# A GRU scan on one core: half of each block copied by ScalarE, a slot of its own for z's last products, a new written order

## The chip, the core and the metric

The kernel runs on one core of one Trainium2 chip. The metric is the time of the device in microseconds (us) for one execution of the whole program; lower is better. The figure given for a kernel is the median of its runs, with the lowest and the highest beside it.

A core has five engines that work side by side, each through its own list of instructions in a fixed order: TensorE (PE; its weight loads are listed apart as PEld), VectorE (DVE), ScalarE (ACT), GpSimd (POOL) and SyncE (SP), which here only issues DMAs. They share SBUF, the large on-chip memory, and PSUM, the accumulators of TensorE (here eight banks). Semaphores tell an engine that another has finished what it needs.

## The reference

```python
def step(h, inp):                       # h: 64 x 512
    x_t, prop = inp
    comb = jnp.concatenate([x_t, h], axis=-1)
    z = jax.nn.sigmoid(comb @ Wz + bz)
    r = jax.nn.sigmoid(comb @ Wr + br)
    comb2 = jnp.concatenate([x_t, r * h], axis=-1)
    h_cand = jnp.tanh(comb2 @ Wh + bh)
    h_new = (1.0 - z) * h + z * h_cand
    h_next = jnp.where(prop, jnp.tanh(h_new @ Wp + bp), h_new)
    return (h_next, h_new)
...
_, ys = jax.lax.scan(step, h0, (xs, do_prop))   # do_prop: every 4th step but the last
...
x = x + ys                              # x: 64 x 128 x 512, float32
```

The batch has 64 sequences of 128 steps, and the input and the state have 512 numbers each. W is 1024 x 512 for each of the three gates (its upper half meets x_t, its lower half h), Wp is 512 x 512. Everything is float32.

## The kernel before

**Two kinds of work.** The products of x with the upper halves of the weights don't depend on the recurrence. They are made in batches of four steps, ahead of time, by a scheme of the Strassen kind: seven products where eight would be plain, nested twice, so that GpSimd first sums blocks of x (`s12r`, `s56`, `o12` and the like, 128 columns each), VectorE and GpSimd have once summed the weights (`weigh`, L560, into `tw`, `tt`, `tf`), and TensorE multiplies sums by sums into four PSUM banks (`ps_q`, `ps_y`, `ps_a`, `ps_x`). ScalarE and VectorE bring the products to SBUF (`mb`); GpSimd adds them up, 768 columns at a time (`pool_add`, L796, 1.83 us each), into a staging tile `st`. The recurrent part, h times the lower halves, has to run step after step.

**Layout.** The batch is cut into two halves, e and l, of 32 rows each. The state of one half is a tile of 128 partitions (four quarters of the 512 features, 32 batch rows each) by 128 columns. Its transpose `hT` is what TensorE takes as the stationary operand. One product of a gate for one half is 16 matmuls of 128 columns, or 8 where half of the features are meant. All matmuls are issued by `mm` (L397), so in the profile they are told apart by their tiles.

**From the staging tile to the place of use.** A block of x's gates leaves GpSimd in `st` with the batch halves on the wrong partitions. `place` (L807) issues four DMAs from SP (L813), 64 partitions by 384 columns each, which put it into `cp`: two of them change the half of the partitions, two keep it. `cp` is what the gates add in.

**One step.** Steps 0 to 3 and 124 to 127 multiply plainly (`gates_plain`). Steps 4 to 123 (`gates_seven`) make r and z of both halves with seven products of 8 matmuls. GpSimd makes the four sums or differences of `hT` for it (`sa`, L999). Four of the products go, one after another, through one PSUM slot, B_ in `ps_b`: the first from `hT` itself, three from `sa`; E_ and A_, R_ are slots in `ps_b`, `ps_e` and `ps_r`. VectorE adds the products and x's part together (`plus`, L1006): for z it forms c3 = E_ + x and ps_z = B_ + c3 for one half, then, after the next product has come into B_, ps_z = B_ + x for the other. Then comes `rest`: ScalarE's sigmoid of z (L955), VectorE's keep = (z - 1) * h (L1043), the products of the third gate from `rhT` into `ps_e` and `ps_r`, tanh into `cand`, and for each half

```python
tensor(lambda h=h, zh=zh: nc.vector.tensor_mul(zh, cand_(t)[:, h, :], zh),
...
tensor(lambda h=h, zh=zh, n=n: nc.vector.tensor_sub(h_(n)[:, h, :], zh, keep_(t)[:, h, :]),
...
turn(hT_(n)[:, h, :], h_(n)[:, h, :], [("h", n, h)], [("hT", n, h)])
```

in the profile L1057, L1071 and, inside `turn`, L908. Here zh is a part of `ps_z`, in PSUM; cand, keep and h are in SBUF. The next step's first product waits for that transpose. After every fourth step, h goes through Wp and tanh first. GpSimd adds h to x (L1088) and SP writes the result to the output.

**What sets the order.** Every operation is announced with what it reads and writes. A table of numbers (`ORDER`) then says in which order all operations are emitted, and each engine runs its own in just that order; the program derives the semaphore waits from the reads and writes. So the products of the batches stand between those of the recurrence at places that the table has fixed. TensorE's list opens with 42 dummy matmuls (`idle`) that need no data. SP's list opens with loads of x (`load_step`, `load_x`) and of the weights (`load_wx` for the upper halves, `load_wh` for the lower ones).

## Time and profile before

| what | value |
|---|---|
| median of 3 runs | 1272.42 us (1270.58 to 1274.52) |
| the profiled execution | 1273.74 us |
| its span, first to last instruction | 1271.9 us |
| mean granted clock of TensorE | 0.998 of full speed |
| PE busy | 1239.7 us, 97%, 37698 instructions |
| PEld busy | 1109.9 us, 87% |
| VectorE busy | 822.3 us, 65%, 2567 instructions |
| ScalarE busy | 677.1 us, 53%, 2063 instructions |
| GpSimd busy | 939.3 us, 74%, 1481 instructions |
| DMA | 95.9 MB, mean 75 GB/s |

The profile's page comes from one execution. Times are in us unless ns is written. A row such as "L796 POOL TENSOR_TENSOR st<-mb,mb 128x768 ... x77 | 141.3, 1834 | 30.2 <-ACT mb L763 24.6" is a group of alike instructions: line 796 of the kernel, the engine, the operation, what is written and what read, partitions by columns, and the count; then the busy time and the mean of one in ns; then how long the engine had stood idle just ahead of them, and what ended most of that. In the view of waits, a row names engine, tile and line that waited, then what released them, with the time in us, the count and the longest. In the timeline a row is start, duration, engine, line and tiles, and in square brackets the wait ahead of it. Consecutive matmuls overlap in the records, so "busy" for TensorE says that one was in flight and not that it ran at its best.

### The profile page before, as it was taken

How to read it: one execution, taken by the hardware profiler on the slowest of the kernel's cores; microseconds unless marked ns; L12 is line 12 of the kernel's file. 1: busy time of each engine (PE TensorE's matmuls, PEld its weight loads, DVE VectorE, ACT ScalarE, POOL GpSimd, SP SyncE). 2: the span in 40 equal slices, each digit the busy share in tenths (PEclk: the TensorE clock that was granted, in tenths of full speed). 3: DMA queues.
4: the chain of work that ended last, by engine and by line, in shares of the span. 5: the costliest groups of instructions: out<-in, count | busy, mean ns of one | idle time of the engine just before them, and what ended most of it. 6: DMA issues, size and time to landing. Idle time of an engine off the chain costs nothing. (4 is left out here: it accounts for less than half of the span.)

```text
span 1271.9 us, 85560 instructions
## 1 busy us (share of the span) xinstructions
PE 1239.7 (97%) x37698; PEld 1109.9 (87%) x37698; DVE 822.3 (65%) x2567; ACT 677.1 (53%) x2063; POOL 939.3 (74%) x1481
## 2 busy tenths in 40 slices
PE   8899999999999999999999999999999999999987
PEld 6788888888889998888889888998988988898877
DVE  4566666666666666666676666666666666666654
ACT  1355655555555555655555555564655555555543
POOL 7767777788677887767878676887777877677851
PEclk9999999999999999999999999999999999999999
DMA  8322232322232332222322232322232322233221
GB/s 217 85 68 64 62 83 66 87 72 63 73 75 69 86 74 68 62 73 76 82 69 64 71 76 76 86 62 71 67 80 71 84 68 61 75 75 77 70 70 37
DMA packets 112002, 95.90 MB, mean 75 GB/s; under 512 B 10891, under 2 KB 107531, under 8 KB 111630
## 3 DMA queue, kind: packets, MB, share of 16 engines
q1 hardware_dynamic: 110760, 89.76, 28.1%
q8 instruction: 296, 4.85, 1.6%
q0 software_dynamic: 512, 0.53, 0.2%
q14 instruction: 76, 0.62, 0.2%
q10 hardware_dynamic: 358, 0.14, 0.0%
HBM read 24.84 MB, written 16.78 MB: 33 GB/s over the span
## 5 line engine op out<-in xcount | busy, mean ns | idle before, releaser
L999 POOL TENSOR_TENSOR sa<-hT 128x64 f32<-128x64 f32 x240 | 75.9, 323 | 119.7 <-DVE hT L908 107.9
L796 POOL TENSOR_TENSOR st<-mb,mb 128x768 f32<-128x768 f32 x77 | 141.3, 1834 | 30.2 <-ACT mb L763 24.6
L397 PE MATMUL ps_b<-wh,sa 128*32 128x128 f32 x3840 | 155.4, 274 | 3.7 <-DVE ps_r L1006 1.6
L1088 POOL TENSOR_TENSOR xj<-xj,h 128x256 f32<-128x256 f32 x127 | 93.7, 738 | 66.3 <-DVE h L1071 65.1
L397 PE MATMUL ps_r<-wh,rhT 128*32 128x128 f32 x4096 | 140.9, 274 | 1.5 <-issue 1.5
L397 PE MATMUL ps_e<-wh,rhT 128*32 128x128 f32 x4096 | 138.9, 273 | 2.0 <-ACT ps_e L951 1.5
L397 PEld LDWEIGHTS ps_b<-wh,sa 128*32 128x32 f32 x3840 | 109.2, 109 | 29.3 <-issue 15.6
L796 POOL TENSOR_TENSOR mb<-mb,mb 128x768 f32<-128x768 f32 x60 | 110.0, 1834 | 32.3 <-ACT mb L763 27.6
L397 PEld LDWEIGHTS ps_e<-wh,rhT 128*32 128x32 f32 x4096 | 117.1, 110 | 8.0 <-DVE rhT L908 2.5
L397 PEld LDWEIGHTS ps_r<-wh,rhT 128*32 128x32 f32 x4096 | 119.5, 110 | 4.2 <-issue 1.9
L908 DVE STREAM_TRANSPOSE hT<-h 128x128 f32<-128x128 f32 x318 | 96.6, 307 | 31.0 <-ACT h L955 19.7
L518 DVE STREAM_TRANSPOSE xT<-xj 128x256 f32<-128x256 f32 x128 | 84.1, 661 | 40.9 <-DMA xj<-in_x_dram 37.3
L397 PE MATMUL ps_y<-tw,s 128*32 128x192 f32 x1456 | 93.6, 326 | 0.0
L1043 DVE SCALAR_TENSOR_TENSOR keep<-ps_z,h 128x256 f32<-128x256 f32 x128 | 54.3, 424 | 57.0 <-ACT ps_z L955 57.0
L796 POOL TENSOR_TENSOR st<-mb 128x768 f32<-128x768 f32 x47 | 86.6, 1842 | 4.7 <-DMA cp<-st 3.2
L397 PE MATMUL ps_e<-wh,hT 128*32 128x128 f32 x2176 | 85.2, 273 | 2.1 <-ACT ps_r L951 1.4
L1057 DVE TENSOR_TENSOR ps_z<-cand,ps_z 128x128 f32<-128x128 f32 x256 | 74.2, 290 | 18.2 <-ACT cand L955 6.8
L999 POOL TENSOR_TENSOR sa<-hT,sa 128x64 f32<-128x64 f32 x240 | 77.5, 323 | 10.8
L951 ACT COPY ps_r<-cp 128x128 f32<-128x128 f32 x256 | 69.5, 271 | 28.0 <-PE ps_r L397 12.3
L908 DVE STREAM_TRANSPOSE rhT<-rh 128x128 f32<-128x128 f32 x256 | 79.2, 309 | 6.8
L397 PE MATMUL ps_b<-wh,hT 128*32 128x128 f32 x1920 | 78.0, 276 | 4.9 <-DVE hT L908 3.5
L955 ACT ACTIVATE ps_z<-ps_z 128x256 f32<-128x256 f32 x128 | 47.1, 368 | 60.6 <-DVE ps_z L1006 53.7
(173 smaller groups left out, 3388.4 us busy)
## 6 DMA issues: line engine op xcount, KB each, us to landing
cp<-st SPq DMA_DIRECT2D x496, 96.0 KB
out_dram<-xj SPq DMA_DIRECT2D x254, 64.0 KB
xj<-in_x_dram SPq DMA_DIRECT2D x248, 64.0 KB
wh<-in_L_cond_Wr_dram SPq DMA_DIRECT2D x4, 256.0 KB
wx<-in_L_cond_Wh_dram SPq DMA_DIRECT2D x2, 512.0 KB
wx<-in_L_cond_Wz_dram SPq DMA_DIRECT2D x2, 512.0 KB
wh<-in_L_cond_Wz_dram SPq DMA_DIRECT2D x4, 256.0 KB
wh<-in_L_cond_Wh_dram SPq DMA_DIRECT2D x4, 256.0 KB
```

The source lines that it names most:

```text
L397: nc.tensor.matmul(dst, lhsT=lhsT, rhs=rhs, start=start, stop=True, skip_group_check=True)
L518: lambda: nc.vector.transpose(out=xT_(g)[:, i].rearrange("p c (a h b) -> p h (c a) b", a=S, h=S), in_=xj(t).rearrange("p h (e k) -> p h k ...
L796: el("pool", 768, lambda: nc.gpsimd.tensor_add(dst, a, b), reads, writes, rank=FOLD)
L908: add("dve", 0.23, lambda: nc.vector.transpose(out=dst, in_=src), reads, writes, land=0.08, main=True)
L951: el("act", n, lambda: nc.scalar.copy(dst, src), reads, writes, "+" + bank, main=True)
L955: el("act", n, lambda: nc.scalar.activation(dst, src, func), reads, writes, used_, main=True)
L999: tensor(lambda: nc.gpsimd.tensor_sub(sa[:, n], a, b), reads, [("sa", t, n)], n=64, engine="pool")
L1043: lambda: nc.vector.scalar_tensor_tensor(out=keep_(t), in0=zz[:, 0:2], scalar=1.0, in1=h_(v), op0=ALU.subtract, op1=ALU.mult),
L1057: tensor(lambda h=h, zh=zh: nc.vector.tensor_mul(zh, cand_(t)[:, h, :], zh), [("cand", t, h), ("z", 0, h)], [("z", 0, h)], "+z")
L1088: el("pool", 256, lambda: nc.gpsimd.tensor_add(x_out, x_out, h_(new_)), [("h", new_, 0), ("h", new_, 1)] + xk_, xk_)
```

## The change

There are five edits, and a new table for the order.

1. **Copies.** `place` issues two DMAs instead of four, for the rows that change the half of the partitions. The rows that keep it are copied by ScalarE, two copies of 64 partitions by 384 columns (line 838 of the changed kernel). 248 DMAs become 248 copies.
2. **A slot for z's last products.** The third and the fourth product from `sa` go to a slot F_ of their own in `ps_z` and no longer to B_. What VectorE adds is split otherwise: w1 = E_ + x, w1 = B_ + w1, w0 = B_ + x, and then z = F_ + w1 for one half and z = F_ + w0 for the other. w0 and w1 stand in the tile of `keep`, and c3 is gone. These are five additions where there were three, in each of 120 steps.
3. **The end of a step.** cand * z is written over cand, in SBUF, and no longer over z in `ps_z`. The subtraction that makes h therefore reads two SBUF tiles, cand and keep. In the last step the addition to the output reads cand in the same way.
4. **The plain last steps.** In steps 124 to 127 ScalarE no longer puts x's part into `ps_z` ahead of z's products. They start from nothing, and VectorE adds x's part behind them, once for each half.
5. **First loads.** The x of steps 4 to 7 is loaded by eight DMAs of 32 partitions ahead of the lower halves of the weights, and the loads at SP's start stand in a written order. The dummies' cost in the planner's numbers is 0.107 instead of 0.22, and there are as many of them as before.

The matmuls are the same in number, 18870 instructions with the dummies. VectorE has 2817 instructions where it had 2569, ScalarE 2318 where it had 2074, GpSimd 1486 in both, and SP 789 where it had 1037.

```diff
 ORDER = """
-c-oD+2YXf7l`Xo~+H38cb2tg8L`AzDu3c@rT+!uNW$bclx7}^KU$<}H?&s9qufuI4f)EHKKp;TmB!K{t6$m0o2oOntkjOzGL>35800DQZ?jLyHIAhK+$Cz
...
+c-kep2Y6N4l_k8-x#!%R^UIG=MOC?~>~d(A$L@CMvMX12*=4)R?y;wBch7W>+hN@PdwTkJ8%anAgb+d?0Rkj)4k9CR6d;6zgvf{}auivl*^gnpz4uyc?{j
...
     add("act", 0.01, lambda: None, [("h_in", 0, q) for q in range(NQ)], [("h", 0, 0), ("h", 0, 1)])
+    for h in range(S):
+        for q in range(NQ):
+            load(
+                "sp",
+                lambda h=h, q=q: nc.sync.dma_start(
+                    out=steps_in[part(q), Q4 : 2 * Q4, h, :], in_=x[ts(h, V), Q4 : 2 * Q4, ts(q, J)]),
+                [("xj", t, h, q) for t in range(Q4, 2 * Q4)], cost=0.47,
+            )
     for i in range(3):
         load_wh(wh[i], gates_in[i][D:], ("wh", 0, i))
+    plan.behind += list(zip(heads, heads[1:]))
+    heads = None
...
         g, i = divmod(t, Q4)
-        if t >= Q4:
+        if t >= 2 * Q4:
             load_x(t)
...
         for h in range(S):
-            for d in range(S):
-                load(
-                    "sp",
-                    lambda h=h, d=d: nc.sync.dma_start(
-                        out=cp_(2 * g + a)[ts(d, B), nb, h].rearrange("p b g u -> p (b g u)"),
-                        in_=st_(n)[ts(h, B), d].rearrange("p b g u -> p (b g u)"),
-                    ),
-                    [("cp", 2 * g + a, b, nb, e, h, d) for b in range(2) for e in range(3)], [("st", n)], size=98.0, cost=0.5,
-                )
+            own = slice(h * B, (h + 1) * B)
+            keys = lambda d: [("cp", 2 * g + a, b, nb, e, h, d) for b in range(2) for e in range(3)]
+            load(
+                "sp",
+                lambda h=h: nc.sync.dma_start(
+                    out=cp_(2 * g + a)[ts(1 - h, B), nb, h].rearrange("p b g u -> p (b g u)"),
+                    in_=st_(n)[ts(h, B), 1 - h].rearrange("p b g u -> p (b g u)"),
+                ),
+                keys(1 - h), [("st", n)], size=98.0, cost=0.5,
+            )
+            el("act", 384, lambda h=h, own=own: nc.scalar.copy(
+                cp_(2 * g + a)[own, nb, h].rearrange("p b g u -> p (b g u)"),
+                st_(n)[own, h].rearrange("p b g u -> p (b g u)")),
+               [("st", n)], keys(h), rank=EVAC)
...
             bank = (ae, rl, zz)[i // NQ % 3]
-            add("pe", 0.22, lambda bank=bank, i=i: nc.tensor.matmul(
+            add("pe", 0.107, lambda bank=bank, i=i: nc.tensor.matmul(
                 bank.rearrange("p a n -> p (a n)")[part(i % NQ)], lhsT=zeros[:, :V], rhs=zeros,
...
     A_, R_ = ae[:, 0], rl[:, 0]
-    B_, E_ = be[:, 0], be[:, 1]
+    B_, E_, F_ = be[:, 0], be[:, 1], zz[:, 2]
     S2, S4 = (wt[:, n] for n in range(2))
...
             reset(t, h)
-        seed(zz[:, 0:2].rearrange("p h (c n) -> p c h n", c=C), g_ap(t)[:, :, :, Z, :],
-             g_keys(t, (Z,)), [("z", 0, 0), ("z", 0, 1)], "z", 256)
+        if t < SEVEN:
+            seed(zz[:, 0:2].rearrange("p h (c n) -> p c h n", c=C), g_ap(t)[:, :, :, Z, :],
+                 g_keys(t, (Z,)), [("z", 0, 0), ("z", 0, 1)], "z", 256)
+            for h in range(S):
+                gate(zz[:, h], hT[:, h], wh[Z], [("hT", v, h), ("z", 0, h)] + wk(Z, 0, 1, 2, 3), [("z", 0, h)], "z")
+            return
         for h in range(S):
-            if t < SEVEN:
-                gate(zz[:, h], hT[:, h], wh[Z], [("hT", v, h), ("z", 0, h)] + wk(Z, 0, 1, 2, 3), [("z", 0, h)], "z")
-                continue
-            product_k(zz[:, h], hT[:, h], wh[Z], ALL[KH:], False, [("hT", v, h), ("z", 0, h)] + wk(Z, 2, 3), [("z", 0, h)], "+z")
+            product_k(zz[:, h], hT[:, h], wh[Z], ALL[KH:], h == 0, [("hT", v, h)] + wk(Z, 2, 3),
+                      [("z", 0, n) for n in range(h, S)], "+z")
             product_k(zz[:, h], hT[:, h], wz, ALL[:KH], False, [("hT", v, h), ("z", 0, h), ("wz", 0, 0), ("wz", 0, 1)], [("z", 0, h)], "+z")
+            tensor(lambda h=h: nc.vector.tensor_add(cn(zz[:, h]), cn(zz[:, h]), xpart(t, Z, h)),
+                   [("z", 0, h)] + g_keys(t, (Z,), (h,)), [("z", 0, h)], "+z")
...
-        def p(ps, name, n, w, keys):
-            product_k(ps, sa[:, n], w, [(0, 0), (1, 1)], False, reads=[("sa", t, n), (name, 0)] + keys,
-                      writes=[(name, 0)], banks="+b")
+        def p(ps, name, n, w, keys, bank="b", start=False):
+            product_k(ps, sa[:, n], w, [(0, 0), (1, 1)], start,
+                      reads=[("sa", t, n)] + ([] if start else [(name, 0)]) + keys,
+                      writes=[(name, 0)], banks="+" + bank)
...
         reset(t, 1)
-        p(B_, "B", 2, wh[Z][:, 0:KH], [("T", 0, 3)])
-        plus(cn(c3_(t)), cn(E_), xpart(t, Z, 1), [("E", 0)] + gx[Z][1], [("c3", t)], "b")
-        plus(zz[:, 1], B_, c3_(t), [("B", 0), ("c3", t)], [("z", 0, 1)], "b +z")
-        p(B_, "B", 3, wh[Z][:, KH:K], wk(Z, 2, 3))
-        plus(cn(zz[:, 0]), cn(B_), xpart(t, Z, 0), [("B", 0)] + gx[Z][0], [("z", 0, 0)], "b +z")
+        w0, w1 = keep_(t)[:, 0, :], keep_(t)[:, 1, :]
+        p(F_, "F", 2, wh[Z][:, 0:KH], [("T", 0, 3)], "z", True)
+        plus(cn(w1), cn(E_), xpart(t, Z, 1), [("E", 0)] + gx[Z][1], [("keep", t, 1)], "b")
+        plus(w1, B_, w1, [("B", 0), ("keep", t, 1)], [("keep", t, 1)], "b")
+        plus(cn(w0), cn(B_), xpart(t, Z, 0), [("B", 0)] + gx[Z][0], [("keep", t, 0)], "b")
+        plus(zz[:, 1], F_, w1, [("F", 0), ("keep", t, 1)], [("z", 0, 1)], "+z")
+        p(F_, "F", 3, wh[Z][:, KH:K], wk(Z, 2, 3), "z")
+        plus(zz[:, 0], F_, w0, [("F", 0), ("keep", t, 0)], [("z", 0, 0)], "+z")
...
             zh = zz[:, h]
-            tensor(lambda h=h, zh=zh: nc.vector.tensor_mul(zh, cand_(t)[:, h, :], zh),
-                   [("cand", t, h), ("z", 0, h)], [("z", 0, h)], "+z")
+            ch, ck = cand_(t)[:, h, :], [("cand", t, h)]
+            tensor(lambda ch=ch, zh=zh: nc.vector.tensor_mul(ch, ch, zh), ck + [("z", 0, h)], ck, "z")
             if last:
                 o = x_out[:, h, :]
-                tensor(lambda o=o, zh=zh: nc.vector.tensor_add(o, zh, o), [("z", 0, h), ("xl", 0, h)], [("xl", 0, h)], "z")
+                tensor(lambda o=o, ch=ch: nc.vector.tensor_add(o, ch, o), ck + [("xl", 0, h)], [("xl", 0, h)])
                 for q in range(NQ):
...
                 continue
-            tensor(lambda h=h, zh=zh, n=n: nc.vector.tensor_sub(h_(n)[:, h, :], zh, keep_(t)[:, h, :]),
-                   [("z", 0, h), ("keep", t)], [("h", n, h)], "z")
+            tensor(lambda h=h, ch=ch, n=n: nc.vector.tensor_sub(h_(n)[:, h, :], ch, keep_(t)[:, h, :]),
+                   ck + [("keep", t, h)], [("h", n, h)])
             turn(hT_(n)[:, h, :], h_(n)[:, h, :], [("h", n, h)], [("hT", n, h)])
```

Three places show what the table moves. On TensorE, the last of the seven-product steps (step 123; wh_64 is the lower half of Wr and wh_65 that of Wz, wh_66 that of Wh, `wx` and `wt` hold the weight sums of r and z; `rhT_103` is the transposed r * h). Before:

```order
L397 MATMUL ps_b<-wh_64,hT_101 32x128 x8
L397 MATMUL ps_r<-wt,hT_101 32x128 x8
L397 MATMUL ps_b<-wx,sa_106 32x128 x8
L397 MATMUL ps_b<-wt,sa_106 32x128 x8
L397 MATMUL ps_e<-wh_64,hT_101 32x128 x8
L397 MATMUL ps_b<-wh_65,sa_106 32x128 x16
L397 MATMUL ps_e<-wh_66,rhT_103 32x128 x16
L397 MATMUL ps_r<-wh_66,rhT_103 32x128 x16
```

And in the changed kernel, where `ps_y`, `ps_x` and `ps_a` are products of a batch:

```order
L401 MATMUL ps_b<-wh_64,hT_101 32x128 x8
L401 MATMUL ps_y<-tw_71,s4r_95 32x192 x4
L401 MATMUL ps_r<-wt,hT_101 32x128 x8
L401 MATMUL ps_b<-wx,sa_106 32x128 x8
L401 MATMUL ps_e<-wh_64,hT_101 32x128 x8
L401 MATMUL ps_z<-wh_65,sa_106 32x128 x8
L401 MATMUL ps_b<-wt,sa_106 32x128 x8
L401 MATMUL ps_a<-tw_71,xT_82 32x192 x4
L401 MATMUL ps_x<-tt,o_0_97 32x192 x4
L401 MATMUL ps_x<-tt,xT_82 32x192 x4
L401 MATMUL ps_z<-wh_65,sa_106 32x128 x8
L401 MATMUL ps_e<-wh_66,rhT_103 32x128 x16
```

Batch products now stand between the products of this step, and the two last of z's products, one piece of 16 into `ps_b` before, are two pieces into `ps_z`, of which the second follows further down.

On VectorE, the same step (the tiles with numbers 98 and 99 are the new and the old h, 104 is keep, 105 cand, 107 c3). Before:

```order
L1006 TENSOR_TENSOR ps_z<-ps_b,c_0_107 128x128
L908 STREAM_TRANSPOSE rhT_103<-rh_102 128x128
L1006 TENSOR_TENSOR ps_z<-ps_b,cp_84 128x128
L1043 SCALAR_TENSOR_TENSOR keep_104<-ps_z,h_99 128x256
L1057 TENSOR_TENSOR ps_z<-cand_105,ps_z 128x128
L1071 TENSOR_TENSOR h_98<-ps_z,keep_104 128x128
L908 STREAM_TRANSPOSE hT_100<-h_98 128x128
L1057 TENSOR_TENSOR ps_z<-cand_105,ps_z 128x128
L1071 TENSOR_TENSOR h_98<-ps_z,keep_104 128x128
```

Now:

```order
L1034 TENSOR_TENSOR keep_104<-ps_b,keep_104 128x128
L1034 TENSOR_TENSOR ps_z<-ps_z,keep_104 128x128
L1034 TENSOR_TENSOR cand_105<-ps_b,cand_105 128x128
L1034 TENSOR_TENSOR ps_r<-ps_b,cand_105 128x128
L1034 TENSOR_TENSOR keep_104<-ps_b,cp_84 128x128
L1034 TENSOR_TENSOR ps_z<-ps_z,keep_104 128x128
L992 TENSOR_TENSOR rh_102<-ps_r,h_99 128x128
L931 STREAM_TRANSPOSE rhT_103<-rh_102 128x128
L1074 SCALAR_TENSOR_TENSOR keep_104<-ps_z,h_99 128x256
L1089 TENSOR_TENSOR cand_105<-cand_105,ps_z 128x128
L1102 TENSOR_TENSOR h_98<-cand_105,keep_104 128x128
L931 STREAM_TRANSPOSE hT_100<-h_98 128x128
```

The two additions from `ps_b` into `ps_z` have become four, two of them from `ps_z`, and the multiplication and the subtraction at the end name cand in the place of ps_z.

On ScalarE, at the last sigmoid of z but few, near the end of the program (`cp_84` is the place of use, `st_88` and `st_89` are staging tiles, 105 is cand). Before:

```order
L763 COPY ps_q<-bias_s 128x384
L763 COPY mb_85<-ps_a 128x2x6x32
L955 ACTIVATE ps_z<-ps_z 128x256
L955 ACTIVATE cand_105<-ps_e 128x128
L951 COPY ps_e<-cp_83 128x128
L955 ACTIVATE cand_105<-ps_r 128x128
```

Now:

```order
L978 ACTIVATE cand_105<-ps_e 128x128
L974 COPY ps_e<-cp_83 128x128
L978 ACTIVATE ps_z<-ps_z 128x256
L781 COPY ps_a<-ps_q 128x384
L838 COPY cp_84<-st_88 64x384
L838 COPY cp_84<-st_89 64x384
L978 ACTIVATE cand_105<-ps_r 128x128
L838 COPY cp_84<-st_89 64x384
```

The copies from the staging tiles stand between the sigmoid of z and the second half's tanh, the row from `ps_r` that makes cand, and one of them behind it.

On SP, the start of the list (`xj` holds x; `wx` is filled with the upper halves of the weights). Before:

```order
L456 DMA wh_64<-in_L_cond_Wr_dram 32x4x512
L425 DMA xj<-in_x_dram 32x2x128
L441 DMA wx<-in_L_cond_Wh_dram 128x2x512
L425 DMA xj<-in_x_dram 32x2x128
L441 DMA wx<-in_L_cond_Wr_dram 128x512
L441 DMA wx<-in_L_cond_Wz_dram 128x2x512
L441 DMA wx<-in_L_cond_Wr_dram 128x512
L441 DMA wx<-in_L_cond_Wr_dram 128x2x512
L435 DMA xj<-in_x_dram 128x1x128
L441 DMA wx<-in_L_cond_Wz_dram 128x2x512
```

Now:

```order
L433 DMA xj<-in_x_dram 32x2x128 x2
L449 DMA wx<-in_L_cond_Wr_dram 128x512 x2
L449 DMA wx<-in_L_cond_Wr_dram 128x2x512
L449 DMA wx<-in_L_cond_Wz_dram 128x2x512 x2
L449 DMA wx<-in_L_cond_Wh_dram 128x2x512 x2
L517 DMA xj<-in_x_dram 32x4x128 x8
L464 DMA wh_64<-in_L_cond_Wr_dram 32x4x512
L443 DMA xj<-in_x_dram 128x1x128
```

The loads of x stand ahead of the weights, those of r's upper half ahead of the others', and the x of steps 4 to 7 behind them.

More of the change, by code (lines that the diff above doesn't have):

```diff
@@ L51, in __init__ @@
         self.first = []
+        self.behind = []
         self.due = -9.0
@@ L407, in el, with load @@
         return add(engine, COST[engine][n], emit, reads, writes, banks, land=LAND[engine], **kw)
-    def load(engine, emit, writes, reads=(), size=64.0, cost=0.45, few=False):
+    heads = []
+    def load(engine, emit, writes, reads=(), size=64.0, cost=0.45, few=False, kind=1):
         op = add(
@@ L415, in load @@
         )
-        op.dma = 2 if engine == "poolq" else 3 if few else 1
+        op.dma = 2 if engine == "poolq" else 3 if few else kind
+        if heads is not None and engine == "sp":
+            heads.append(op.index)
         return op
@@ L1045, in rest @@
             ),
-            zk + [("h", v, 0), ("h", v, 1)], [("keep", t)], "z", 256,
+            zk + [("h", v, 0), ("h", v, 1)], [("keep", t, 0), ("keep", t, 1)], "z", 256,
         )
         if last:
-            el("pool", 256, lambda: nc.gpsimd.tensor_sub(x_out, x_out, keep_(t)), [("keep", t)] + xk_, xk_ + [("xl", 0, 0), ("xl", 0, 1)], main=True)
+            el("pool", 256, lambda: nc.gpsimd.tensor_sub(x_out, x_out, keep_(t)), [("keep", t, 0), ("keep", t, 1)] + xk_, xk_ + [("xl", 0, 0), ("xl", 0, 1)], main=True)
         versions[0] += 1
```

270 lines of the change are left out of this document (137 added, 133 removed), and 2 rows, old and new, of the table RINGS.

## The prediction

> **What bounds the kernel now.** First the busy time of the engines by stretch: the opening, the long middle, the last steps.
>
> ```profile
> core 0: us, PE busy (x) PEld busy (x) DVE busy (x) ACT busy (x) POOL busy (x), PEclk, DMA share, GB/s
> 0.00:60.00 60.00, 48.89 (x1270) 40.15 (x1274) 29.29 (x54) 12.61 (x36) 43.95 (x62) 0.97 0.62 157
> 60.00:1225.00 1165.00, 1154.24 (x35233) 1036.81 (x35225) 769.11 (x2432) 647.82 (x1971) 880.69 (x1401) 1.00 0.29 72
> 1225.00:1272.00 47.00, 36.53 (x1215) 32.94 (x1208) 23.85 (x82) 16.66 (x57) 14.66 (x19) 0.97 0.20 49
> ```
>
> In the middle TensorE shows no matmul for 10.8 of 1165 us; the opening has 11.1 us without one, the end 10.5. The change leaves the matmuls as they are, so it can act on the time in two ways only: through what TensorE waits for, and through the two ends. A busy TensorE hides waits, since a matmul is shown for 0.27 us while the next starts 0.03 us later. So next I read the waits of TensorE and of its weight loads.
>
> ```profile
> PEld ps_b L397 <- DVE hT L908: 24.8, 63, 0.9
> PEld ps_b L397 <- issue: 18.4, 71, 1.5
> PE ps_b L397 <- DVE hT L908: 3.5, 11, 0.6
> ```
>
> The first product of a step (into ps_b, from hT, the transposed state) waits for the transpose in 63 of the 120 steps that have it. The recurrence, not only the amount of work, decides when TensorE goes on. One step in order of time shows its last links:
>
> ```profile
> 806.40 0.65 PE L397 MATMUL ps_b<-wh,sa 128*32 128x128 f32 x16
> ...
> 807.10 0.30 DVE L1006 TENSOR_TENSOR ps_z<-ps_b,c 128x128 f32<-128x128 f32 x1 [0.30 <-PE ps_b L397]
> ...
> 807.55 0.64 PE L397 MATMUL ps_b<-wh,sa 128*32 128x128 f32 x16
> ...
> 808.25 0.30 DVE L1006 TENSOR_TENSOR ps_z<-ps_b,cp 128x128 f32<-128x128 f32 x1 [0.85 <-PE ps_b L397]
> ...
> 808.39 1.83 POOL L796 TENSOR_TENSOR st<-st,mb 128x768 f32<-128x768 f32 x1
> ...
> 808.58 0.37 ACT L955 ACTIVATE ps_z<-ps_z 128x256 f32<-128x256 f32 x1 [1.36 <-DVE ps_z L1006]
> ...
> 808.98 0.42 DVE L1043 SCALAR_TENSOR_TENSOR keep<-ps_z,h 128x256 f32<-128x256 f32 x1 [0.43 <-ACT ps_z L955]
> ...
> 809.44 0.30 DVE L1057 TENSOR_TENSOR ps_z<-cand,ps_z 128x128 f32<-128x128 f32 x1
> ...
> 809.84 0.29 DVE L1071 TENSOR_TENSOR h<-ps_z,keep 128x128 f32<-128x128 f32 x1
> ```
>
> z's last product, its addition, sigmoid, keep, the multiplication, the subtraction that makes h, then the transpose: each link waits for the one before it.
>
> **The change, part by part.**
>
> *The subtraction that makes h.* Today it reads ps_z (PSUM) and keep (SBUF). Changed, it reads cand and keep, both in SBUF, 254 times, always just ahead of the transpose that TensorE waits for; behind it on VectorE stand that transpose and the other half's multiplication and subtraction. VectorE instructions with two SBUF inputs are rare in this trace (the weight sums, L560), so their rows give the price; the third and fourth row are GpSimd's at the same time:
>
> ```profile
> 43.20 0.92 DVE L560 TENSOR_TENSOR tw<-tw,wx 128x768 f32<-128x768 f32 x1
> 46.99 1.77 DVE L560 TENSOR_TENSOR tw<-wx,tw 128x768 f32<-128x768 f32 x1
> ...
> 46.93 1.01 POOL L560 TENSOR_TENSOR tt<-tw,tt 128x384 f32<-128x384 f32 x1
> 47.89 1.18 POOL L594 TENSOR_TENSOR s<-xT 128x128 f32<-128x128 f32 x1
> ...
> L594 POOL TENSOR_TENSOR s<-o 128x128 f32<-128x128 f32 x60 | 27.7, 462 | 1.8 <-PE ps_x L397 1.1
> L1071 DVE TENSOR_TENSOR h<-ps_z,keep 128x128 f32<-128x128 f32 x254 | 71.2, 283 | 9.3
> ```
>
> Alone the instruction took 0.92 us. Started 0.06 us behind a GpSimd instruction that ran until 47.94, it took 1.77: 0.95 of waiting and 0.82 of its own. The GpSimd instruction behind it then took 1.18 instead of 0.46. So the two engines take turns, a whole instruction at a time. Today's subtraction shows nothing of that: at 809.84 it took 0.29 us in the middle of a GpSimd addition that ran until 810.22. Changed, it would have waited 0.38 us there.
>
> How much in all? GpSimd is 74% busy:
>
> ```profile
> L796 POOL TENSOR_TENSOR st<-mb,mb 128x768 f32<-128x768 f32 x77 | 141.3, 1834 | 30.2 <-ACT mb L763 24.6 <-DVE rhT L908 3.0 <-DMA cp<-st 0.9
> L796 POOL TENSOR_TENSOR mb<-mb,mb 128x768 f32<-128x768 f32 x60 | 110.0, 1834 | 32.3 <-ACT mb L763 27.6 <-DVE mb L787 3.0 <-DVE rhT L908 1.0
> L796 POOL TENSOR_TENSOR st<-mb 128x768 f32<-128x768 f32 x47 | 86.6, 1842 | 4.7 <-DMA cp<-st 3.2 <-PE ps_r L397 0.7
> L796 POOL TENSOR_TENSOR st<-st,mb 128x768 f32<-128x768 f32 x30 | 55.0, 1833 | 3.6 <-ACT mb L763 3.4
> L999 POOL TENSOR_TENSOR sa<-hT 128x64 f32<-128x64 f32 x240 | 75.9, 323 | 119.7 <-DVE hT L908 107.9 <-PE ps_b L397 6.8 <-DVE h L1071 4.6
> ```
>
> A subtraction that came at random would meet a 1.83 us addition in 31% of cases (392.9 of 1271.9 us) and wait 0.92 us, and a shorter instruction in 43% and wait about 0.25: 0.39 us each, 99 us in all. That is the upper end. The lower end is nothing, where GpSimd stands idle; the last row says that it often does just then, waiting for hT. Laid over GpSimd's rows, 165 of the 254 subtractions start inside one of its instructions, and the rest of it averages 0.24 us over all 254, 62 us in all. I take this value, since the row above is of the very place.
>
> What reaches TensorE: the two batch halves of a step are computed in parallel, so at most one half's wait counts fully, some 127 x 0.24 = 30 us. In half of the steps TensorE waits for hT already and nothing hides it; in the others there are some tenths of a us. With the new order's slack (next item) I take 22 us, and 4 for the other half and the engines behind: +26.
>
> The Trainium skill ("SBUF — State Buffer", section "Who interferes with whom") has a rule for this: a VectorE instruction with two SBUF inputs and a GpSimd instruction that reads SBUF exclude each other for the whole instruction. By that rule a wait can reach 1.8 us, behind one of the long additions; the rows above show 0.95 us at most. Capped at 0.95, the average falls from 0.24 to about 0.23 us and the sum by 1 us.
>
> *z's own slot and its order.* Today the third and fourth product of ps_b must wait until VectorE has read the one before (807.10, then 807.55). Changed, one of these two waits is gone, the other stays. From start to start, such blocks of 16 come 12 us late in total; the visible part is 3.7 us, and the idle time of their weight loads, 29.3 against 4.3 and 4.8 for the two neighbour groups of half the count, bounds it by 29.3 - 9.1 = 20 us:
>
> ```profile
> L397 PE MATMUL ps_b<-wh,sa 128*32 128x128 f32 x3840 | 155.4, 274 | 3.7 <-DVE ps_r L1006 1.6 <-DVE ps_z L1006 1.0 <-POOL sa L999 0.5
> L397 PEld LDWEIGHTS ps_b<-wh,sa 128*32 128x32 f32 x3840 | 109.2, 109 | 29.3 <-issue 15.6 <-POOL st L796 2.4 <-POOL sa L999 1.9
> L397 PEld LDWEIGHTS ps_b<-wt,sa 128*32 128x32 f32 x1920 | 57.1, 110 | 4.3 <-issue 1.3 <-POOL sa L999 0.6 <-POOL s12r L594 0.3
> L397 PEld LDWEIGHTS ps_b<-wx,sa 128*32 128x32 f32 x1920 | 56.3, 110 | 4.8 <-POOL sa L999 2.0 <-issue 1.5
> ```
>
> I take -7 (0 to -14). The new order also puts more work between z's last product and the next step's first: at the durations of the rows (16 matmuls of 128 columns 0.44 us, 8 of 192 0.33) the median rises from 2.8 to 3.0 us, the upper quartile from 3.5 to 3.7. That takes some of the waiting for hT away: -6 (0 to -10).
>
> *ScalarE's copies and two more additions.* 248 copies of 384 columns at 0.485 us (its copies from bias_s, below) are 120 us on an engine that is 53% busy; two more additions per step on VectorE, 240 x 0.30 = 72 us, at 65%.
>
> ```profile
> L763 ACT COPY ps_y<-bias_s 128x384 f32<-128x384 f32 x63 | 30.5, 485 | 13.9 <-DVE mb L787 11.8 <-DVE cp L706 2.0
> ```
>
> Both engines have room. But a copy waits for GpSimd's addition into st, and behind it in ScalarE's order stand sigmoids and tanhs; today only SP's queue waits there. The ends: 0 if st is always early, 12 us if a tenth of the 124 pairs holds a tanh for 1 us. I take +4. The 248 fewer DMAs give nothing: in the middle the engines for them are 29% busy.
>
> *The opening.*
>
> ```profile
> 9.00 1.08 PE L397 MATMUL ps_x<-wx,xT 128*32 128x128 f32 x16 [3.35 <-DVE xT L518]
> ...
> 19.62 1.46 PE L397 MATMUL ps_x<-wx,xT 128*32 128x128 f32 x44
> ...
> 38.35 0.86 PE L397 MATMUL ps_q<-wx,xT 128*32 128x192 f32 x16 [1.98 <-ACT ps_q L763]
> ...
> 49.91 0.86 PE L397 MATMUL ps_y<-tf,s12r 128*32 128x192 f32 x16 [2.21 <-ACT ps_y L763]
> ...
> 36.79 0.63 DVE L518 STREAM_TRANSPOSE xT<-xj 128x256 f32<-128x256 f32 x1 [4.14 <-DMA xj<-in_x_dram]
> ```
>
> The first product starts at 9.00, with 16 matmuls taking 0.85 us, twice the 0.027 us each of 19.62, and that lasts until 17: 4 us lost. Changed, x and the weights that come first are first in the queue, the dummies run closer to the first product, and x of steps 4 to 7 stands ahead of the recurrent weights (its transposes wait 4.14 us at 36.79). I take -7 (2 us of earlier start, 3 of slow matmuls, 2 of the later gaps), from +2 if a weight that was moved back is now late, to -13.
>
> *The end.* In the last two steps before the plain ones nothing stands between the products of a step; changed, 8 batch products of 0.33 us do, and fill gaps there that sum to 4.5 us: -2.6, less a little, since z's seed in the four plain steps becomes an addition of 0.30 us behind its products, where VectorE now idles for up to a us before z is used:
>
> ```profile
> 1254.57 0.30 DVE L1057 TENSOR_TENSOR ps_z<-cand,ps_z 128x128 f32<-128x128 f32 x1 [1.09 <-ACT cand L955]
> ```
>
> -2.5 (0 to -5). The lock costs nothing after 1240, where GpSimd is idle.
>
> **Sum.** The profiled execution took 1273.7 us (span 1271.9), 1.3 above the median of 1272.4. -7 -2.5 -7 -6 +26 +4 = +7.5: 1281.2 for that execution, 1280 against the median.
>
> **Rivals.** *Faster:* GpSimd has ended its instruction when h is due, so the lock costs 4 instead of 26; for it speaks that the row of sa shows GpSimd idle for 107.9 us before hT. 1272.4 - 18.5 + 4 = 1258. It decides below about 16 us of lock on the path. *Much slower:* the new order lets the subtractions meet GpSimd at random, 99 us of waiting, of which 60 show: 1272.4 - 18.5 + 60 = 1314. Against it: GpSimd's queue is of the same make as before. *No change:* gains and lock cancel (lock of 15 to 22): 1272.
>
> **How the numbers follow.** A measurement here tells a change from none above about 0.3%, 3.8 us. My forecast (slower, 1277 to 1297) has 0.44, much slower 0.15, no change 0.12, faster 0.29. So slower 0.59. The range 1254 to 1312 reaches into both outer cases and leaves 2 in 10 out.
>
> **What would show it.** The row of the subtraction h<-cand,keep shows above 0.4 us on average, where it now has 0.283, with single ones near 2 us; GpSimd's short instructions rise as well. If it stays near 0.29, the lock is not there and I am wrong on the main term. The weight loads of the first product should wait for hT longer than 24.8 us. The products now in ps_z should show less idle time ahead than the 3.7 and 29.3 us of today, the first product should start at about 7 us, and the last steps should show fewer gaps. ScalarE waiting for st ahead of its copies, with a tanh behind, shows the fourth term.

## The result, and the profile after

The changed kernel takes 1259.62 us (median of 4 runs, 1258.69 to 1259.72), the kernel before 1271.62 (median of 4, 1270.58 to 1274.52). The ratio is 0.9900, 95% interval 0.9882 to 0.9918: faster by 12 us, where the forecast was 1280, slower. The profiled execution took 1259.72 us, its span is 1257.9.

The same three stretches as in the prediction, with the last 47 us and the first 60 cut off again (columns as there):

```profile
0.00:60.00 60.00, 50.82 (x1386) 41.59 (x1390) 28.98 (x57) 14.24 (x41) 37.51 (x56) 1.00 0.64 160
60.00:1211.00 1151.00, 1131.13 (x35012) 1039.95 (x35007) 845.27 (x2662) 753.92 (x2202) 887.35 (x1406) 1.00 0.20 52
1211.00:1258.00 47.00, 39.60 (x1316) 35.79 (x1308) 28.32 (x98) 20.17 (x66) 16.49 (x20) 0.98 0.19 50
```

In the middle TensorE now shows no matmul for 19.9 us (1151 - 1131.13), where it was 10.8, and yet the middle is shorter. So time without any matmul has gone up while time in which matmuls started late has gone down. The groups tell which is which:

```profile
L401 PE MATMUL ps_z<-wh,sa 128*32 128x128 f32 x3840 | 154.2, 273 | 0.1
...
L1102 DVE TENSOR_TENSOR h<-cand,keep 128x128 f32<-128x128 f32 x254 | 127.8, 503 | 11.1
...
L401 PEld LDWEIGHTS ps_z<-wh,sa 128*32 128x32 f32 x3840 | 116.6, 110 | 8.2 <-issue 1.4 <-DVE wh L578 0.4 <-POOL sa L1026 0.4
...
L401 PEld LDWEIGHTS ps_b<-wx,sa 128*32 128x32 f32 x1920 | 57.7, 110 | 2.5 <-POOL sa L1026 1.0
...
L401 PEld LDWEIGHTS ps_b<-wt,sa 128*32 128x32 f32 x1920 | 57.0, 110 | 3.0 <-issue 0.4 <-POOL sa L1026 0.2 <-POOL xj L1119 0.2
```

And in the view of waits:

```profile
PEld ps_b L401 <- DVE hT L931: 24.2, 34, 1.5
...
PE ps_b L401 <- DVE hT L931: 12.7, 20, 1.2
```

The subtraction that makes h takes 503 ns on average and not 283: 56 us more over 254 of them, about what was forecast for the lock (62). z's last products no longer wait (0.1 and 8.2 us of idle time where 3.7 and 29.3 stood). The weight load of a step's first product waits for hT in 34 steps, not 63, but longer at a time: up to 1.5 us, where 0.9 was the longest. Its sum is the same (24.2 us, 24.8 before), while the wait of the matmuls themselves rises from 3.5 to 12.7 us. GpSimd hardly shows the lock: its four rows of 128 columns for `s` take 470 ns on average where they took 466. So the waiting falls on VectorE, and the rise of GpSimd's short instructions, which the prediction named as a sign, is not there.

One long wait in order of time:

```profile
1020.31 1.82 POOL L814 TENSOR_TENSOR st<-mb 128x768 f32<-128x768 f32 x1
...
1020.53 1.76 DVE L1102 TENSOR_TENSOR h<-cand,keep 128x128 f32<-128x128 f32 x1
...
1022.39 0.31 DVE L931 STREAM_TRANSPOSE hT<-h 128x128 f32<-128x128 f32 x1
...
1022.75 0.38 PEld L401 LDWEIGHTS ps_b<-wh,hT 128*32 128x32 f32 x16 [1.55 <-DVE hT L931]
1022.75 0.64 PE L401 MATMUL ps_b<-wh,hT 128*32 128x128 f32 x16 [1.17 <-DVE hT L931]
```

VectorE's subtraction starts 0.22 us behind GpSimd's addition and ends 0.16 us behind its end; the transpose and TensorE follow at once. The longest of the 254 took 1.97 us. The chain that ended last gives VectorE 8% of the span (the shares listed come to 83%):

```profile
PE 71%; DVE 8%; ACT 2%; issue 1%; POOL 1%; DVEq 0%; ACTq 0%; POOLq 0%
```

### The profile page after: what moved, and what is told of

It is laid out like the page before. It is cut to its first block, busy times and chain, and to the rows that moved or that the text cites. A ratio compares the mean times of both kernels' runs of the same rounds, so it can differ in the third digit from the quotient of the medians.

```text
span 1257.9 us, 85383 instructions
## 1 busy us (share of the span) xinstructions
PE 1221.6 (97%) x37698; PEld 1117.3 (89%) x37698; DVE 902.6 (72%) x2815; ACT 788.3 (63%) x2307; POOL 941.4 (75%) x1481
## 4 chain that ended last, share of the span: by engine, by line
PE 71%; DVE 8%; ACT 2%; issue 1%; POOL 1%; DVEq 0%; ACTq 0%; POOLq 0%
PE ps_e L401 13%; PE ps_r L401 11%; PE ps_b L401 11%; PE ps_x L401 8%; PE ps_y L401 8%; PE ps_q L401 8%; PE ps_z L401 7%; PE ps_a L401 4%; DVE h L1102 3%; DVE hT L931 1%; DVE keep L1074 1%; DVE cand L1089 1%; ACT ps_z L978 1%; DVE ps_z L1034 1%; POOL st L814 0%
## 5 line engine op out<-in xcount | busy, mean ns | idle before, releaser
L401 PE MATMUL ps_z<-wh,sa 128*32 128x128 f32 x3840 | 154.2, 273 | 0.1
L838 ACT COPY cp<-st 64x384 f32<-64x384 f32 x248 | 125.9, 509 | 23.8 <-DVE keep L1034 9.1
L401 PE MATMUL ps_r<-wh,rhT 128*32 128x128 f32 x4096 | 138.1, 273 | 0.6 <-DVE rhT L931 0.5
L1102 DVE TENSOR_TENSOR h<-cand,keep 128x128 f32<-128x128 f32 x254 | 127.8, 503 | 11.1
L401 PEld LDWEIGHTS ps_z<-wh,sa 128*32 128x32 f32 x3840 | 116.6, 110 | 8.2 <-issue 1.4
L1034 DVE TENSOR_TENSOR keep<-ps_b,cp 128x128 f32<-128x128 f32 x240 | 66.8, 281 | 36.1 <-PE ps_b L401 34.3
L1034 DVE TENSOR_TENSOR ps_z<-ps_z,keep 128x128 f32<-128x128 f32 x240 | 70.7, 295 | 29.5 <-PE ps_z L401 23.8
L401 PE MATMUL ps_b<-wh,hT 128*32 128x128 f32 x1920 | 77.8, 274 | 12.9 <-DVE hT L931 12.7
L1089 DVE TENSOR_TENSOR cand<-cand,ps_z 128x128 f32<-128x128 f32 x256 | 70.0, 274 | 25.6 <-ACT ps_z L978 13.3
```

The source lines that it names most:

```text
L401: nc.tensor.matmul(dst, lhsT=lhsT, rhs=rhs, start=start, stop=True, skip_group_check=True)
L838: el("act", 384, lambda h=h, own=own: nc.scalar.copy(cp_(2 * g + a)[own, nb, h].rearrange("p b g u -> p (b g u)"), st_(n)[own, h].rearrang ...
L1034: tensor(lambda: nc.vector.tensor_add(dst, a, b), reads, writes, used_)
L1089: tensor(lambda ch=ch, zh=zh: nc.vector.tensor_mul(ch, ch, zh), ck + [("z", 0, h)], ck, "z")
L1102: tensor(lambda h=h, ch=ch, n=n: nc.vector.tensor_sub(h_(n)[:, h, :], ch, keep_(t)[:, h, :]), ck + [("keep", t, h)], [("h", n, h)])
```

## The experiments

Each kernel was timed in five rounds beside the kernel before, on the same chip; ratios are against that. The kernel before had medians of 1275.1, 1275.5 and 1274.7 us in the three sets, 3 to 4 above the 1271.6 of the first comparison, so differences between runs are taken from ratios, at 1275 us to the whole, where they come from different sets.

### The lock alone, in the new order and in the old

In the changed kernel, cand * z goes back into PSUM, to slots that are free there:

```diff
-            ch, ck = cand_(t)[:, h, :], [("cand", t, h)]
-            tensor(lambda ch=ch, zh=zh: nc.vector.tensor_mul(ch, ch, zh), ck + [("z", 0, h)], ck, "z")
+            ch = zz[:, 3 - h]
+            ck = [("F", 0)] if h else [("M", 0)]
+            tensor(lambda ch=ch, zh=zh, h=h: nc.vector.tensor_mul(ch, cand_(t)[:, h, :], zh),
+                   [("cand", t, h), ("z", 0, h)], ck, "+z")
```

> The changed kernel with its own written order, but cand * z goes back into PSUM (a free slot of ps_z for one half, the slot of z's last products for the other), so that no subtraction h reads two SBUF tiles. Theory A (hidden): in the changed kernel the subtraction takes 0.503 us on average and not 0.283, 56 us in all, but TensorE has other products to run meanwhile and hardly any of it reaches the end; without it the kernel takes 1255 to 1260 us (changed kernel: 1259.6). Theory B (paid, as the forecast had it): 22 to 26 us of the 56 reach the end and the other edits gave more than forecast; then 1234 to 1240 us. Under both the row of the subtraction falls back to about 0.28 us.

Measured: 1235.94 us, ratio 0.9701 (0.9680 to 0.9721). Theory B holds: the lock costs the changed kernel 24 us by the medians, 25 by the ratios (0.9900 - 0.9701 of 1275). This run's group of the subtraction:

```profile
L1104 DVE TENSOR_TENSOR h<-ps_z,keep 128x128 f32<-128x128 f32 x254 | 72.9, 287 | 12.0 <-ACT ps_z L974 0.9
```

its wait of the first product's weight load for hT:

```profile
PEld ps_b L401 <- DVE hT L931: 5.7, 27, 0.3
```

the chain that ended last:

```profile
PE 97%; DVE 1%; issue 1%; DMA 1%; ACT 0%; POOL 0%; DVEq 0%; ACTq 0%; POOLq 0%
```

and its middle stretch, cut as above:

```profile
60.00:1187.00 1127.00, 1125.71 (x35004) 1042.51 (x34996) 805.61 (x2662) 752.87 (x2201) 881.54 (x1405) 1.00 0.20 53
```

Without the lock the wait for hT shrinks to 5.7 us, 0.3 at the longest, TensorE makes up 97% of the chain, and in the whole middle it shows no matmul for 1.3 us only. This version beats both kernels.

The other way round, the kernel before with the third edit of the change alone (the lines are those of the change's own diff):

```diff
-            tensor(lambda h=h, zh=zh: nc.vector.tensor_mul(zh, cand_(t)[:, h, :], zh),
+            tensor(lambda ch=ch, zh=zh: nc.vector.tensor_mul(ch, ch, zh), ck + [("z", 0, h)], ck, "z")
```

> The kernel before, with its own order, and one edit alone: cand * z goes to SBUF and the subtraction h reads two SBUF tiles. Theory A1 (the wait is hidden wherever it comes): 1271 to 1276 us. Theory A2 (hidden only in the new order, which leaves room for it): the old order pays, 1285 to 1298 us (1272 plus the forecast's 22 to 26, or half of that). Under both the row of the subtraction rises to about 0.5 us on average.

Measured: 1289.02 us, ratio 1.0109 (1.0087 to 1.0131), 14 us slower, at the low end of A2. Its groups of the subtraction and of the first product's weight load:

```profile
L1071 DVE TENSOR_TENSOR h<-cand,keep 128x128 f32<-128x128 f32 x254 | 125.1, 495 | 8.0
...
L397 PEld LDWEIGHTS ps_b<-wh,hT 128*32 128x32 f32 x1920 | 52.5, 109 | 39.0 <-DVE hT L908 36.5
```

The lock has the same size here (495 ns), and the wait for hT is up from 24.8 to 36.5 us. By the ratios it costs 14 us here and 25 in the new order. So the new order left no room for the lock; as I read it, it took out waits beside which part of the lock passed unseen, but that is argued and not shown.

### Is it the whole instruction of GpSimd?

GpSimd's additions of 768 columns, each split in two:

```diff
-        el("pool", 768, lambda: nc.gpsimd.tensor_add(dst, a, b), reads, writes, rank=FOLD)
+        def halves_():
+            for n in range(2):
+                nc.gpsimd.tensor_add(dst[:, n], a[:, n], b[:, n])
+
+        el("pool", 768, halves_, reads, writes, rank=FOLD)
```

> The changed kernel, h from SBUF, with each of GpSimd's 214 additions of 768 columns split into two of 384. Theory (a subtraction waits for the whole instruction that GpSimd is in): no subtraction takes more than about 1.3 us where single ones took 1.97, the average falls from 0.503 to about 0.40, and since the long waits are what reaches TensorE the kernel takes 1245 to 1253 us. Rival (the wait is for GpSimd's whole run of instructions, or GpSimd's added time, some 20 us, holds up the batches): 1258 to 1270 us.

> As the run in which h is made from PSUM (1235.9 us), with GpSimd's additions of 768 columns split into two. Without a lock there is nothing to be won by it: 1236 to 1240 us, what GpSimd's longer work costs. Then the split's 1252.7 us with h from SBUF are a gain against the long waits alone. Rival (short additions help in another way, say by letting the sums of hT start sooner): 1226 to 1233 us.

Measured: with h from SBUF 1252.72 us, ratio 0.9818 (0.9790 to 0.9846); with h from PSUM 1241.54, ratio 0.9729 (0.9704 to 0.9754), a little above the expected 1236 to 1240. The groups of the first of these:

```profile
L816 POOL TENSOR_TENSOR st<-mb,mb 128x384 f32<-128x384 f32 x154 | 153.4, 1015 | 20.1 <-ACT mb L781 17.3 <-DVE ps_z L1038 2.2 <-DVE cand L1038 0.5
...
L1106 DVE TENSOR_TENSOR h<-cand,keep 128x128 f32<-128x128 f32 x254 | 110.3, 434 | 11.0
```

and in its view of waits the wait for hT, down from 24.2 us:

```profile
PEld ps_b L401 <- DVE hT L935: 9.7, 21, 1.0
```

Halves of 1.0 us bring the mean from 503 to 434 ns and the kernel down by 0.8%, although the split itself seems to cost 0.3% (0.9729 against 0.9701, two intervals that overlap). Without GpSimd's long instructions the lock costs 0.9% (0.9818 against 0.9729) where it cost 2.0%. Counted over the single rows, subtractions that waited more than 0.6 us (over 885 ns long) held 34 of the 56 us before the split and 10 of 38 after it. The expected longest of 1.3 us was missed once; see the end.

### An even delay in the place of the lock

One more VectorE instruction ahead of each subtraction, its result unused; in the changed kernel, as shown here, and in the one with h from PSUM, where it reads `ch` in the place of `zz[:, 3]`:

```diff
+            def later(h=h, ch=ch, n=n):
+                nc.vector.tensor_sub(junk, zz[:, 3], keep_(t)[:, h, :])
+                nc.vector.tensor_sub(h_(n)[:, h, :], ch, keep_(t)[:, h, :])
```

> The changed kernel with one more VectorE instruction of about 0.28 us (PSUM and SBUF operands, its result unused) ahead of each of the 254 subtractions h: a further 71 us on VectorE at the same place, without a lock. It measures how much room is left there. Theory A with plenty of room: 1260 to 1268 us. Theory A with the room used up, or theory B: one half of each step counts, 127 x 0.28 = 36 us, 1285 to 1296 us.

> As the run in which h is made from PSUM (1235.9 us), with one more VectorE instruction of about 0.28 us ahead of each of the 254 subtractions, 71 us in all, evenly. Theory (an even delay mostly fits beside TensorE's other products, it is the uneven long waits that reach the end): 1238 to 1246 us, a smaller share of 71 us than the 23.7 of 56 that the lock costs. Rival (a delay of h costs the same whatever its shape): 0.42 of 71, 1262 to 1270 us.

Measured: on top of the lock 1271.25 us, ratio 0.9972 (0.9960 to 0.9985), 0.7% above the changed kernel and between the two expectations (against 1271.6 us it would be 1268, the upper edge of the first); with h from PSUM 1259.16, ratio 0.9873 (0.9851 to 0.9895), 1.7% or 22 us above 1235.9. The second kernel's group of the added instruction:

```profile
L1106 DVE TENSOR_TENSOR junk<-ps_z,keep 128x128 f32<-128x128 f32 x254 | 73.0, 287 | 8.1 <-ACT ps_z L975 0.9
```

and its wait for hT:

```profile
PEld ps_b L402 <- DVE hT L932: 13.9, 42, 0.6
```

73 us spread evenly cost 22, 0.30 of each us; the lock's 56 cost 25, 0.44 (by the medians alone 0.32 and 0.42). The 38 us that the split leaves cost 0.9%, 11 us, again 0.30. So long waits seem to cost more for their size, but an even delay doesn't hide either: my theory of 1238 to 1246 was wrong, and so was the rival's 1262 to 1270, from the other side. On the chain of h there is little room for anything. On top of the lock the same delay costs only 9 us: a step that already waits for GpSimd pays less for it (the subtraction's mean falls from 503 to 477 ns there).

### Where the other 38 us come from

Without the lock the changed kernel is 38 us below the one before (0.0299 of 1275). The two structural edits were put into the kernel before, under its own order: z's slot (the change's own lines, with the two further additions placed beside the old ones), ScalarE's copies at the places of the DMAs, and both. The copies' edit:

```diff
             for d in range(S):
+                if d == h:
+                    el("act", 384, lambda h=h, d=d: nc.scalar.copy(
+                        cp_(2 * g + a)[ts(d, B), nb, h].rearrange("p b g u -> p (b g u)"),
+                        st_(n)[ts(h, B), d].rearrange("p b g u -> p (b g u)")),
...
+                    continue
                 load(
                     "sp",
...
```

> The kernel before, with its own order, and one edit alone: z's last two products go to a slot of their own in ps_z, with the two further additions on VectorE per step that this takes, one put behind the addition into ps_r and one behind the first addition into ps_z. Theory C (the slot is the gain): products late by 12.1 us in total start on time, 1260 to 1266 us. Rival D (what is won there is waited for at the next transpose, since the recurrence sets the pace): 1268 to 1273 us, with a longer wait of ps_b's weight load for hT than 24.8 us.

> The kernel before, with its own order, and one edit alone: of each block's four DMAs the two that keep their rows become copies by ScalarE, at the same places of the order. Theory E (the copies gain only with an order that brings the sums close to their use, which the old order does not): 1270 to 1277 us. Rival (a block that arrives some 2 us sooner is a gain in any order): 1255 to 1268 us. Rival (ScalarE stands waiting for GpSimd's sum with sigmoids and tanhs behind it, since the places were made for a DMA queue): 1280 us and above.

> The kernel before, with its own order, and two edits: copies by ScalarE, and the slot of its own for z's last products (alone 0.9973 of the time before, 3 us less). What is left to the run in which h is made from PSUM (1235.9 us) is the written order, the first loads and the plain last steps. Theory E (both edits are worth little until the order uses them): 1265 to 1275 us. Rival (the edits themselves are the gain): 1240 to 1255 us.

Measured: the slot alone 1270.97 us, ratio 0.9973 (0.9959 to 0.9987); the copies alone 1286.06, ratio 1.0080 (1.0058 to 1.0102); both 1282.02, ratio 1.0054 (1.0035 to 1.0073). In the old order the two edits together cost 7 us, outside both expectations; I had put them at a small gain.

With the slot alone, the weight loads' groups of z's products and of the step's first product read:

```profile
L401 PEld LDWEIGHTS ps_z<-wh,sa 128*32 128x32 f32 x3840 | 112.5, 109 | 22.4 <-issue 10.7 <-DVE ps_z L1011 1.9 <-POOL sa L1003 1.3
...
L401 PEld LDWEIGHTS ps_b<-wh,hT 128*32 128x32 f32 x1920 | 51.3, 109 | 28.5 <-DVE hT L912 25.7
```

29.3 us fall to 22.4, and the wait for hT rises from 24.8 to 25.7. The time is rival D's, but its reason is hardly shown: less than 1 of the 7 us won at z comes back at the transpose, and the gain is 3. With the copies alone, whose time is that of the third expectation, ScalarE is late with z, as the forecast feared for the copies. The wait of keep for the sigmoid, in the kernel before:

```profile
DVE keep L1043 <- ACT ps_z L955: 57.0, 122, 1.8
```

and with the copies, above the wait for hT:

```profile
DVE keep L1049 <- ACT ps_z L961: 67.9, 122, 2.8
...
PEld ps_b L397 <- DVE hT L914: 32.8, 70, 1.0
```

Then the same edits undone in the new order, with h from PSUM: four DMAs for the copies, and the old slot (where the order has z's third product ahead of an addition that must have read the slot, it is held back).

```diff
-            el("act", 384, lambda h=h, own=own: nc.scalar.copy(
...
+            load("sp", lambda h=h, own=own: nc.sync.dma_start(
...
-        p(F_, "F", 2, wh[Z][:, 0:KH], [("T", 0, 3)], "z", True)
+        p(B_, "B", 2, wh[Z][:, 0:KH], [("T", 0, 3)])
```

> As the run in which h is made from PSUM (1235.9 us), with ScalarE's 248 copies put back to 248 DMAs of SP at the same places of the order. The forecast's term (copies hold up sigmoids and tanhs): 1230 to 1234 us. Rival 1 (both have room): 1235 to 1238 us. Rival 2 (a DMA arrives later than a copy, and the new order counts on the copy): 1240 to 1250 us.

> As the run in which h is made from PSUM (1235.9 us), but z's last two products go to the old slot in ps_b again, with three additions where there were five; where the written order has the third product ahead of the addition that must have read the slot, it is held until then, and so is what needs it. Theory C2 (the slot by itself is what the order lives from): 1250 to 1260 us. Rival (the slot saves the 8 to 10 us of its own waits and the rest is the order): 1243 to 1248 us. Rival (the slot is worth the 3 to 4 us that it gave in the old order): 1238 to 1241 us.

Measured: four DMAs 1276.00 us, ratio 1.0000 (0.9977 to 1.0023); the old slot 1335.70, ratio 1.0465 (1.0438 to 1.0493). Both are far outside what I expected. First the view of waits of the run with DMAs. In the run with copies the row of xT has 13.3 us, and the other three have 0.4, 0.4 and 0.2:

```profile
DVE xT L536 <- DMA xj<-in_x_dram: 30.7, 14, 8.8
...
ACT ps_e L974 <- DMA cp<-st: 23.8, 18, 2.5
...
POOL st L814 <- DMA cp<-st: 20.7, 11, 3.6
ACT ps_r L974 <- DMA cp<-st: 19.7, 14, 4.7
```

and the groups of z's products in the run with the old slot:

```profile
L405 PE MATMUL ps_b<-wh,sa 128*32 128x128 f32 x3840 | 156.2, 276 | 49.5 <-DVE ps_z L1038 29.0 <-DVE ps_r L1038 15.8 <-POOL s L615 1.5
...
L405 PEld LDWEIGHTS ps_b<-wh,sa 128*32 128x32 f32 x3840 | 102.4, 109 | 96.9 <-issue 41.9 <-DVE ps_r L1038 15.4 <-DVE ps_z L1038 6.6
```

The new order uses a block right after its sum, and a copy of 0.51 us is there in time where a DMA is waited for by up to 4.7 us. In the run with DMAs the loads of x, which stand in SP's list too, are late as well (first row), so whether the transfer itself takes longer than the copy or SP's list holds it back is not told apart. The new order also sets z's last two products closely behind the others, which only a slot of their own allows. So in the old order the edits are worth -3 and +10 us, and the new order is no gain without either of them (+38 and +97 us against the run with h from PSUM; of the 97, what comes from holding products back and so disturbing the order is not told apart). What is shown is the sum: the order, with the first loads and the plain last steps, turns 1282 into 1236. Cut as in the account below, 39 of the 48 us between the two profiled executions lie in the middle, 6 in the opening and 2 at the end. The order without the edits could not be tried by itself, since it is written for them.

### The first product

It started at 10.96 us, later than the 9.00 before, where 7 was forecast: ScalarE's queue issues its second quarter of x behind three rows of biases. The changed kernel's row:

```profile
10.96 1.94 PE L401 MATMUL ps_x<-wx,xT 128*32 128x128 f32 x32 [2.92 <-DVE xT L536]
```

Moved ahead of the biases:

```diff
+        order.remove(self.late)
+        order.insert(order.index(self.lead) + 1, self.late)
```

> As the run in which h is made from PSUM (1235.9 us), and in the opening ScalarE's queue issues its second quarter of the first x ahead of the three rows of biases, no longer behind them at 2.47 us. Theory: the first product waits for that quarter (10.96 us against 9.00 before the change), so it starts at 8 to 9 us and the end moves by as much: 1233 to 1235 us. Rival: the weights of r or the later loads of the opening set the pace, the end stays at 1236 us.

Measured: 1238.58 us, ratio 0.9705 (0.9680 to 0.9731), the same as without it (0.9701). In order of time:

```profile
8.76 1.94 PE L404 MATMUL ps_x<-wx,xT 128*32 128x128 f32 x32 [0.84 <-DVE xT L540]
```

The first product starts 2.2 us sooner and the end doesn't move, as the rival had it: the opening is not paced by it.

## Why the prediction was wrong, point by point

For the account the spans are cut at the start of the first product from `sa` (step 4; its weight load) and at the end of the 301st transpose of h. TensorE's lost time is summed over the blocks that came late: the time from the start of one block to the start of the next, beyond 0.0272 us for each matmul row of 128 columns and 0.0407 for each of 192. (The profile lists a matmul of the program as two rows and a dummy as one: 37698 rows for 18870 instructions.)

| part | forecast | measured, changed kernel | measured, h from PSUM |
|---|---|---|---|
| opening, up to step 4 | -7 | -4.2 | -4.9 |
| middle | slot -7, order -6, copies +4, lock +26: +17 | -6.1 | -29.7 |
| end | -2.5 | -3.6 | -3.2 |
| span | +7.5 | -14.0 | -37.8 |

**The lock** was right, and so was what reaches TensorE of it: +26 forecast, 24 to 25 measured, 56 us on VectorE where 62 was taken. The subtraction's mean of 0.503 us is above the 0.4 that was named as its sign. The longest of them, 1.97 us, is a wait of 1.69 behind an addition of 1.81, where the rows before had shown 0.95 at most. The rule of the Trainium skill ("SBUF — State Buffer", section "Who interferes with whom"), that a VectorE instruction with two SBUF inputs and a GpSimd instruction that reads SBUF exclude each other for the whole instruction, agrees with these waits. Splitting the additions is the test of it.

**The rival "faster"** came closest in time (1258), but by luck, since its mechanism is not what happened: the lock was not hidden, it was paid; the gains were larger. That the stated range, 1254 to 1312, holds 1259.6 is owed to the same luck, for it was drawn to reach into this rival.

**The step that failed** is the worth of the new order in the middle: -7, -6 and +4, together -9, measured -29.7 without the lock. TensorE's lost time in the middle was 41.8 us before and is 14.8 with h from PSUM. Ahead of the step's first product it falls from 15.5 to 1.6, so -14 where I had -6 (0 to -10). The comparison behind the -6 was sound: the work between z's last product and the next first product has a median of 3.04 us now against 2.82, while hT comes about as long after that product as before (2.6 to 2.7 us). But these 0.22 us count in each of the 63 steps that waited, 14 us, and I took less than half; that this is why is worked out from the medians and fits the 14 measured, but no run tests it alone. Ahead of z's last products it falls from 9.8 to 1.6, -8 for the -7 forecast. Another 5 us are small groups (products of the third gate, r's sums), which I had left out. So of the 21 us by which the -9 fell short, about 8 are missing at the first product, 1 at z, 5 in these groups and 4 are the cost of the copies, which this account doesn't show in the new order; some 3 are not placed.

**The copies** were judged with the old order in mind. There +10 is what they cost (the forecast's bounds were 0 to 12). In the changed kernel ScalarE waits for GpSimd's sum ahead of 15 copies, 8.6 us in all and 1.7 at the longest, so the sign named for this term is there; what it costs TensorE is not told apart. "The 248 fewer DMAs give nothing: in the middle the engines for them are 29% busy" was the wrong argument: with the DMAs back the engines for them are 29% busy again in the middle, and what needs the blocks waits, so not that load counts but when a block arrives, and in the new order that is worth 38 us.

**Opening and end** went the forecast's way, the opening for other reasons: its first product came later, not sooner, and the run that moved it shows that it doesn't matter. Which of the loads gave the 4 us stays open.

In sum, the middle's gains were about 20 us too small, with the lock right to 2: +7.5 instead of -14.0.

## What to carry to other kernels

A written order and the edits it was made for are one change: price the order by the waits that it takes away step by step, for each waiting step the full shift, and not the edits under the old order. When a change bundles a gain with a known cost, ask whether the cost can be taken out alone; here an operand moved back to PSUM gave 24 to 25 us more. And on a recurrence's chain, keep VectorE's instructions to one SBUF input while GpSimd runs long instructions, or make these shorter.

## What the runs showed of the hardware that was not expected

In the prediction VectorE and GpSimd took turns. In the run with split additions one subtraction took 2.25 us, some 2 of them waiting, while GpSimd ran four instructions through and began a fifth (the timeline of that run):

```profile
841.42 2.25 DVE L1106 TENSOR_TENSOR h<-cand,keep 128x128 f32<-128x128 f32 x1
...
841.56 0.46 POOL L610 TENSOR_TENSOR s<-o 128x128 f32<-128x128 f32 x1
...
841.97 0.46 POOL L613 TENSOR_TENSOR s<-o,s 128x128 f32<-128x128 f32 x1
...
842.38 0.45 POOL L611 TENSOR_TENSOR s<-s,o 128x128 f32<-128x128 f32 x1
...
842.80 0.45 POOL L612 TENSOR_TENSOR s<-o 128x128 f32<-128x128 f32 x1
843.21 0.31 POOL L611 TENSOR_TENSOR s4r<-s4r,xT 128x64 f32<-128x64 f32 x1
```

It was one of 254 in that run; all others took at most 1.2 us. The two longest of the changed kernel, 1.97 and 1.94 us, show the same on a smaller scale: they began within the last 0.04 us of one GpSimd instruction, and the next one, an addition of 1.8 us, still went first. What decides who goes first when GpSimd's instructions follow each other without a gap stays open.
